# A two-layer graph network on one core: GpSimd's order written by hand in both layers, with the clearing of a short row at three places among the gathers of every group

## The chip, the cores and the metric

The kernel runs on one core of one Trainium2 chip. A core has five engines that work side by side, each on its own queue of instructions: TensorE (PE in the profile, with its weight loads as PEld), VectorE (DVE), ScalarE (ACT), GpSimd (POOL) and SyncE (SP), which issues most of the plain DMAs. GpSimd issues the indirect DMAs, the ones that fetch rows of a table by a list of row numbers. The metric is the device time of one execution in microseconds, and the time of a kernel is the median over its runs.

## The reference

There are 6250 nodes with 256 features and 200000 edges, each with a source node, a destination node and 128 features. The edges come sorted by destination. Two layers follow each other, each added to its input and normalised:

```python
edge_index = jnp.stack([src, dst])
x = _layernorm(x + _L0_gnn_ref(x, edge_index, edge_attr_128, W_edge, b_edge, W1, b1, W2, b2, eps, gamma, beta))
x = _layernorm(x + _L1_gnn_ref(x, W, att, src, dst))
```

The first layer makes a message for every edge, sums the messages by destination, and sends the sums through two dense layers and a normalisation over all nodes:

```python
msg = relu(x[src] + edge_attr @ W_edge + b_edge)
agg = segment_sum(msg, dst)
h = relu(((1 + eps) * x + agg) @ W1 + b1) @ W2 + b2
h = relu((h - mean(h)) * rsqrt(var(h) + 1e-5) * gamma + beta)
```

The second layer is attention with four heads. Every edge gets a logit from its two ends, the logits are made into weights by a softmax over the edges of one destination, and the weighted rows of the sources are summed:

```python
e = leaky_relu(es[src] + ed[dst])
alpha = exp(e - segment_max(e, dst)[dst]) / segment_sum(exp(...), dst)[dst]
out = segment_sum(alpha * z[src], dst)
```

So both layers need, for every edge, one row of a table of nodes: `x[src]` in the first, `z[src]` in the second.

## The kernel before

**Tiling.** The 200000 edges are cut into 1563 rows of 128 edges (`NSUB`), and 14 rows make a group (`S = 14`). There are 112 groups (`G`); the last has 9 rows. One row is fetched by one indirect DMA: 128 row numbers, one for each partition, and a table row for each. So each layer issues 1563 gathers on GpSimd.

**The first layer.** Rows are taken in pairs. `fetch` (L537 to L544, the gather itself at L542) takes a buffer `xg` from a pool of 14 and issues one or two gathers into it, from `in_x` in the first 20 groups and from `xb_tab`, a copy of `x` with the bias added, in all later ones. `features` multiplies the edge features by `W_edge` on TensorE into `pt`. `sums` (L556) adds the gathered rows on VectorE. `upper` (L561, ScalarE) and `lower` (L565, VectorE) make the relu in two parts, and `add_up` (L575) sums by destination with a one-hot matrix on TensorE. At the end of a group `flush` carries the sums through the dense layers. While groups 3 to 19 run, `biased` (L497 to L502) also writes `xb_tab` piece by piece: a load, an addition on VectorE (L500), a store.

**Between the layers.** `middle` finishes the normalisation, writes the tables `z_tab` and `ed_tab`, and uses GpSimd for a few additions (L727).

**The second layer.** `gather` (L877 to L886, the gather itself at L883) issues the gathers of one group into `ring`, which has room for four groups. The gathers of group i+1 stand in the program in front of the work on group i. `logits` (L951 to L963) needs the whole gathered group, and its first reader of it is the addition at L952. Then come maxima, the weights, and `weigh` (L1007 on VectorE, L1011 on TensorE), which multiplies the gathered rows by the weights and sums them by destination. `leave` normalises the finished rows and stores them; the last two groups are stored by an indirect DMA on GpSimd (L1039).

**What sets the order.** Both loops stand in a block whose engines run in the order in which the program is written:

```python
with tc.manual_schedule(engines={ET.DVE, ET.PE, ET.Activation, ET.SP}):
```

GpSimd (`ET.Pool`) is not in that set, so a planner orders its queue. In both loops GpSimd has nothing but the gathers and, at the very end, the two stores. An engine's instructions start in the order of its queue, and an instruction waits on semaphores for the buffers that it needs.

Of the kernel before, what the change touches and what calls it, by code (L numbers as in the profile page):

```python
# [6 lines left out]
F32 = mybir.dt.float32  # L7
# [6 lines left out]
ET = mybir.EngineType  # L14
# [18 lines left out]
XB_FROM = 20  # L33
RING = 4
XTB = 4
FIRST = 256
IN_RANGE = "the value is an id of a node, which the kinds of inputs bound"

# [10 lines left out]
def gnn(ctx, tc, io, N, E):  # L49
    nc = tc.nc  # L50
# [16 lines left out]
    const = ctx.enter_context(tc.tile_pool(name="const", bufs=1))  # L67
# [40 lines left out]
    nc.vector.memset(nil, 0.0)  # L108
    ones3 = const.tile([3, P], BF16, name="ones3")
    nc.vector.memset(ones3, 1.0)  # L110


    gf = const.tile([P, 2 * G], F32, name="gf")
# [325 lines left out]
    with ExitStack() as st:  # L439
# [97 lines left out]
        def fetch(k):  # L537
            g, j0, w = pairs_[k]
            XG[k] = gp.tile([P, 2, D], F32, tag="xg", name="xg")
            for i in range(w):  # L540
                t = gs[g] + j0 + i
                nc.gpsimd.indirect_dma_start(  # L542
                    out=XG[k][:, i, :], out_offset=None, in_=io["x"] if g < GB else xb_tab,
                    in_offset=bass.IndirectOffsetOnAxis(ap=src_sb[:, t:t + 1], axis=0))  # L544

        def features(k):
            g, j0, w = pairs_[k]
            pt = PT[k] = pe.tile([P, 2, D], F32, tag="pe", name="pt")
            for i in range(w):
                if g < GB:  # L550
                    nc.tensor.matmul(pt[:, i, :], ones3, bias3, start=True, stop=False)
                nc.tensor.matmul(pt[:, i, :], EA.pop(gs[g] + j0 + i), we_sb, start=not g < GB, stop=True)  # L552
# [32 lines left out]
            while chunks:  # L585
                yield from biased(chunks.pop(0))

        with tc.manual_schedule(engines={ET.DVE, ET.PE, ET.Activation, ET.SP}):
            def run(gen):
                for _ in gen:  # L590
                    pass

            run(positions(0, ldp))
            pieces(0)
            run(hot(0))
            load_rest()
            XW[0] = window(0)

            side = [positions(r, ldp) for r in range(1, len(parts))]
            rest = [first_table()]  # L600
            checks = [order(r, ldp) for r in range(len(parts))]
            hots, flushes = iter(()), []
            fill = zeros()
            extras = [place_rows(t0, pps, wk) for t0 in range(0, NSUB, P)]
            for f in (0, 1):
                if f < K:
                    fetch(f)
                    features(f)

            def step(queue):  # L610
                while queue:
                    if next(queue[0], True) is None:
                        return True
                    queue.pop(0)
                return False

            for k in range(K + 2):
                g = pairs_[min(k, K - 1)][0]
                if k < K and pairs_[k][1] == 0:
                    hots = hot(g + 1) if g + 1 < G else iter(())  # L620
                    if g % 2 == 0 and g + 2 < G:
                        pieces(g // 2 + 1)
                    if g + 1 < G:
                        XW[g + 1] = window(g + 1)
                    if g == GB - 1:
                        while step(rest):
                            pass
                j = k - firsts_[g] if k < K else 99
                if k + 2 < K:
                    fetch(k + 2)  # L630
                    features(k + 2)
                if k < K:
                    sums(k)
                    upper(k)
                    if 1 <= k:
                        lower(k - 1)
                elif k == K:
                    lower(k - 1)
                if k >= 2:
                    add_up(k - 2)  # L640
                    if k - 2 in lasts_:
                        run(fill)
                        gg = pairs_[k - 2][0]
                        flushes.append(flush(gg, ACC.pop(gg), XW.pop(gg)))
                        if gg > TG and extras:
                            flushes.append(extras.pop(0))
                if k == min(2, K - 1):
                    places_rest()
                if j >= 3:
                    next(hots, None)  # L650
                if k < K and pairs_[min(k + 1, K - 1)][0] != g:
                    run(hots)
                if k < 7:
                    next(fill, None)
                step(flushes)
                if len(flushes) > 1:
                    step(flushes)
                step(side)
                if 3 <= g < GB and k < K:
                    step(rest)  # L660
                    step(rest)
                if g >= GB:
                    step(checks)
                if k < K and g == TG and pairs_[k][1] == 0:
                    while step(side):
                        pass
                    while step(checks):
                        pass
                    flushes.append(tables(pps, wk))
                    extras = [break_columns(), break_rows(pps, wk)] + extras  # L670
            for q in (side, rest, checks, flushes, extras):
                while step(q):
                    pass
# [3 lines left out]
    def middle(h2T, stats):  # L677

        with ExitStack() as st:
# [28 lines left out]
            nc.sync.dma_start(ed_tab[NB * P:], zero[:, 0, :EW])  # L708
            cuts = [0] + [min(c0, NB * P) for c0 in range(FIRST, NB * P + CH, CH)]
            cs = list(zip(cuts, cuts[1:]))  # L710
            M = {}

            def load(ci):
                c0, c1 = cs[ci]
                xt = yp.tile([P, 2, CH], F32, tag="xt", name="xt", bufs=XTB)
                nc.sync.dma_start(xt[:, :, :c1 - c0], io["xT"].rearrange("(k p) n -> p k n", p=P)[:, :, c0:c1])
# [76 lines left out]
            none = iter(())  # L793
            for ci in range(min(XTB - 1, nch)):
                load(ci)
            with tc.manual_schedule(engines={ET.DVE, ET.PE, ET.Activation, ET.SP}):
                for i in range(nch + 3):
                    if i + XTB - 1 < nch:
                        load(i + XTB - 1)
                    a, b, d = (f(j) if 0 <= j < nch else none  # L800
# [45 lines left out]
    with ExitStack() as st:  # L846
# [30 lines left out]
        def gather(g):  # L877
            n = size(g)
            slot = T["slot"] if T["slot"] + n <= RING * S else 0
            T["slot"] = slot + n  # L880
            zg = ring[:, slot:slot + n]
            for j, t in enumerate(groups(g)):
                nc.gpsimd.indirect_dma_start(  # L883
                    out=zg[:, j, :], out_offset=None, in_=z_tab,
                    in_offset=bass.IndirectOffsetOnAxis(ap=src_sb[:, t:t + 1], axis=0))
            T["zg", g] = zg  # L886

        def loads(g):
# [155 lines left out]
            n = size(g)  # L1044
            return [(j, min(2, n - j)) for j in range(0, n, 2)]

        with tc.manual_schedule(engines={ET.DVE, ET.PE, ET.Activation, ET.SP}):
            gather(0)
            loads(0)
            loads(min(1, G - 1))  # L1050
            places(0)
            dst_parts(0)
            none = iter(())

            for i in range(G + 2):
                units = pairs(i - 1) if 1 <= i <= G else []
                hot = onehots(i) if i < G else none
                out = none
                if i + 1 < G:
                    gather(i + 1)  # L1060
                if 1 < i + 2 < G:
                    loads(i + 2)
                if 1 <= i <= G:
                    load_h(i - 1)
                    maxima(i - 1)
                if i + 1 < G:
                    places(i + 1)
                next(hot, None)

                def some(k):  # L1070
                    for _ in range(min(k, len(units))):
                        weigh(i - 1, *units.pop(0))

                some(1)
                if i < G:
                    logits(i)
                some(1)
                if i >= 2:
                    carry(i - 2)
                    out = leave(i - 2)  # L1080
                if i + 1 < G:
                    dst_parts(i + 1)
                some(1)
                next(out, None)
                some(1)
                if i < G:
                    rows_between(i)
                next(hot, None)
                some(1)
                next(out, None)  # L1090
                some(1)
                for _ in out:
                    pass
                some(len(units))
                for _ in hot:
                    pass
# [217 lines left out]
```

## Time and profile before

| what | value |
|---|---|
| median of 11 runs | 4111.64 us (4105.77 to 4126.58) |
| the profiled execution, its own time | 4113.03 us |
| its span, first to last instruction | 4111.2 us |
| PE busy | 2944.6 us, 72% of the span |
| DVE busy | 3178.8 us, 77% |
| ACT busy | 1041.9 us, 25% |
| POOL busy | 3010.8 us, 73%, 3158 instructions |
| first gather of the first layer starts | 3.0 us |
| last gather of the first layer starts | 1992.6 us |
| first gather of the second layer starts | 2099.1 us |
| last gather of the second layer starts | 4069.6 us |

The table's last four rows are starts of instructions in the trace, in microseconds from the start of the span. A busy time is the sum of an engine's instructions; an engine that is less than fully busy can still be the one that sets the pace, if the rest of its time is a fixed pause between instructions. In the lists of groups a line reads: source line, engine, operation, what is written and read, shapes, count, then busy time and mean duration in nanoseconds of one, then the idle time in front of these instructions and what ended it. In a timeline a line reads: start and duration in microseconds, engine, line, operation, and in brackets the idle time before it with what ended that. A list of waits gives, for an engine, what waited for what: microseconds in total, times, and the longest one.

### The profile page before, as it was taken

How to read it: one execution, taken by the hardware profiler on the slowest of the kernel's cores; microseconds unless marked ns; L12 is line 12 of the kernel's file. 1: busy time of each engine (PE TensorE's matmuls, PEld its weight loads, DVE VectorE, ACT ScalarE, POOL GpSimd, SP SyncE). 2: the span in 40 equal slices, each digit the busy share in tenths (PEclk: the TensorE clock that was granted, in tenths of full speed). 3: DMA queues.
4: the chain of work that ended last, by engine and by line, in shares of the span. 5: the costliest groups of instructions: out<-in, count | busy, mean ns of one | idle time of the engine just before them, and what ended most of it. 6: DMA issues, size and time to landing. Idle time of an engine off the chain costs nothing. (4 is left out here: it accounts for less than half of the span.)

```text
span 4111.2 us, 49111 instructions
## 1 busy us (share of the span) xinstructions
PE 2944.6 (72%) x12883; PEld 2001.8 (49%) x12883; DVE 3178.8 (77%) x8203; ACT 1041.9 (25%) x3046; POOL 3010.8 (73%) x3158
## 2 busy tenths in 40 slices
PE   7899787777777777777746666666666666666665
PEld 4456665556665666665533433333333343333333
DVE  6677988877777777777757777778777777777787
ACT  3233333333333333333421111111111111111111
POOL 7567777777777777777557777777777777777774
PEclk9799999998999999999877777777777777777777
DMA  6755655555555555555565555555555555555553
GB/s 204 220 165 169 196 173 169 169 166 172 167 161 162 160 165 167 167 167 163 158 167 150 144 149 151 151 150 145 149 150 150 151 150 145 150 151 151 150 147 94
DMA packets 298029, 656.24 MB, mean 160 GB/s; under 512 B 86827, under 2 KB 170139, under 8 KB 290572
## 3 DMA queue, kind: packets, MB, share of 16 engines
q0 software_dynamic: 150144, 416.54, 36.4%
q1 hardware_dynamic: 146090, 235.43, 16.9%
q8 instruction: 106, 1.74, 0.2%
q14 instruction: 183, 1.50, 0.1%
q10 hardware_dynamic: 1506, 1.04, 0.1%
HBM read 617.82 MB, written 34.99 MB: 159 GB/s over the span
## 5 line engine op out<-in xcount | busy, mean ns | idle before, releaser
L883 POOL DMA_INDIRECT ring<-z_tab,src_sb x1563 | 1495.6, 957 | 495.7 <-issue 293.6
L542 POOL DMA_INDIRECT xg<-xb_tab,src_sb x1283 | 1214.9, 947 | 390.9 <-issue 274.8
L1011 PE MATMUL acc<-y,oh 128*128 128x260 f32 x3126 | 1071.4, 477 | 296.9 <-DVE y L1007 295.8
L552 PE MATMUL pt<-we_sb,ea_t 128*128 128x256 f32 x3126 | 946.3, 420 | 308.0 <-DVE hl L565 302.5
L1011 PEld LDWEIGHTS acc<-y,oh 128*128 128x128 f32 x3126 | 645.2, 228 | 541.5 <-DVE y L1007 460.7
L552 PEld LDWEIGHTS pt<-we_sb,ea_t 128*128 128x128 f32 x3126 | 563.8, 201 | 515.6 <-DVE hl L565 201.6
L561 ACT ACTIVATE hl<-pt 128x512 fp32r<-128x512 f32 x782 | 466.8, 597 | 1070.0 <-DVE pt L556 966.4
L556 DVE TENSOR_TENSOR pt<-pt,xg 128x512 f32<-128x512 f32 x782 | 542.0, 693 | 218.1 <-DMA xg<-xb_tab,src_sb 200.8
L575 PE MATMUL acc<-hl,oh 128*128 128x512 f32 x1563 | 668.6, 510 | 1.9 <-DVE hl L565 1.9
L565 DVE SCALAR_TENSOR_TENSOR hl<-pt,hl 128x512 fp32r<-128x512 f32 x782 | 532.9, 682 | 0.0
L1007 DVE TENSOR_TENSOR y<-ring,cst 128x520 f32<-128x520 f32 x782 | 527.8, 675 | 0.6 <-PE acc L1011 0.4
L542 POOL DMA_INDIRECT xg<-in_x,src_sb x280 | 265.8, 949 | 121.5 <-issue 64.5
L575 PEld LDWEIGHTS acc<-hl,oh 128*128 128x128 f32 x1563 | 312.8, 200 | 50.1 <-DVE hl L565 2.6
L962 PE MATMUL tr<-consts,top 128*4 128x128 f32 x112 | 41.5, 371 | 398.8 <-DVE top L944 398.8
L952 DVE TENSOR_TENSOR e<-e,ring 128x56 f32<-128x56 f32 x112 | 28.6, 255 | 347.5 <-DMA ring<-z_tab,src_sb 277.0
L1023 ACT COPY ag<-acc 128x260 f32<-128x260 f32 x111 | 41.6, 375 | 875.8 <-DVE acc L1020 875.1
L523 DVE TENSOR_TENSOR oh<-iota_p,dloc 128x896 fp32r<-128x896 f32 x224 | 241.5, 1078 | 0.0
L933 DVE TENSOR_TENSOR oh<-cst,dloc 128x896 f32<-128x896 f32 x224 | 239.3, 1068 | 0.2 <-ACT cst L993 0.2
L962 PEld LDWEIGHTS tr<-consts,top 128*4 128x4 f32 x112 | 9.2, 82 | 458.3 <-issue 440.7
L414 DVE SCALAR_TENSOR_TENSOR pmk<-p,mk 128x128 f32<-128x128 f32 x224 | 56.3, 289 | 126.6 <-ACT h2T L404 125.4
L400 PEld LDWEIGHTS p<-r,w_sb 128*128 128x128 f32 x896 | 137.4, 220 | 13.8 <-ACT r L395 1.7
L390 PE MATMUL p<-hw,w_sb 128*128 128x128 f32 x896 | 127.0, 288 | 22.8 <-DVE carry L472 22.1
(219 smaller groups left out, 3060.2 us busy)
## 6 DMA issues: line engine op xcount, KB each, us to landing
ea_t<-in_eaT SPq DMA_DIRECT2D x54, 1792.0 KB
dlb<-dl_tab SPq DMA_DIRECT2D x111, 448.0 KB
ring<-z_tab,src_sb POOLq DMA_INDIRECT x1563
xg<-xb_tab,src_sb POOLq DMA_INDIRECT x1283
xw<-in_x SPq DMA_DIRECT2D x112, 128.0 KB
hw<-hT_tab SPq DMA_DIRECT2D x112, 128.0 KB
out<-o SPq DMA_DIRECT2D x110, 128.0 KB
xr<-in_x SPq DMA_DIRECT2D x24, 256.0 KB
```

The source lines that it names most:

```text
L400: nc.tensor.matmul(p2[:, m, :], w2_sb[:, k, m * P:(m + 1) * P], r1[:, k, :], start=(k == 0), stop=(k == 1))
L523: nc.vector.tensor_tensor(OH[g][:, c0:c1], iota_p.unsqueeze(1).to_broadcast([P, c1 - c0, P]), dl.unsqueeze(2).to_broadcast([P, c1 - c0, P] ...
L542: nc.gpsimd.indirect_dma_start(out=XG[k][:, i, :], out_offset=None, in_=io["x"] if g < GB else xb_tab, in_offset=bass.IndirectOffsetOnAxis ...
L552: nc.tensor.matmul(pt[:, i, :], EA.pop(gs[g] + j0 + i), we_sb, start=not g < GB, stop=True)
L556: nc.vector.tensor_add(PT[k][:, :w], PT[k][:, :w], XG.pop(k)[:, :w])
L561: nc.scalar.activation(HL[k][:, :w, 0], PT[k][:, :w], AF.Relu)
L565: nc.vector.scalar_tensor_tensor(HL[k][:, :w, 1], PT.pop(k)[:, :w], 0.0, HL[k][:, :w, 0].bitcast(F32), op0=OP.max, op1=OP.subtract)
L575: nc.tensor.matmul(ACC[g].rearrange("p a d -> p (a d)"), OH[g][:, j0 + i], hl[:, i].rearrange("p a d -> p (a d)"), start=(j0 + i == 0), st ...
L883: nc.gpsimd.indirect_dma_start(out=zg[:, j, :], out_offset=None, in_=z_tab, in_offset=bass.IndirectOffsetOnAxis(ap=src_sb[:, t:t + 1], axi ...
L933: nc.vector.tensor_tensor(T["oh", g][:, c0:c1], iota_p.unsqueeze(1).to_broadcast([P, c1 - c0, P]), dloc[:, gs[g] + c0:gs[g] + c1].unsqueez ...
L1007: nc.vector.tensor_tensor(y[:, :w], T["zg", g][:, j0:j0 + w, :ZW].rearrange("p s (h f) -> p s h f", f=F + 1), by_edge(T["ex", g], g)[:, j0 ...
L1011: nc.tensor.matmul(T["acc", g].rearrange("p h f -> p (h f)"), T["oh", g][:, j0 + i, :], y[:, i].rearrange("p h f -> p (h f)"), start=(j0 + ...
```

## The change

GpSimd joins the engines whose order is that of the program, in both layers. A new tile of one partition and 768 float32 values is set to zero on GpSimd after the gathers of rows 4, 9 and 13 of every group (rows are counted from 0). Nothing reads this tile.

```diff
+RESTS = (4, 9, 13)
...
+    rest_t = const.tile([1, 768], F32, name="rest_t")
+
+    def breathe():
+
+        nc.gpsimd.memset(rest_t, 0.0)
...
                 nc.gpsimd.indirect_dma_start(
                     out=XG[k][:, i, :], out_offset=None, in_=io["x"] if g < GB else xb_tab,
                     in_offset=bass.IndirectOffsetOnAxis(ap=src_sb[:, t:t + 1], axis=0))
+                if j0 + i in RESTS:
+                    breathe()
...
-        with tc.manual_schedule(engines={ET.DVE, ET.PE, ET.Activation, ET.SP}):
+        with tc.manual_schedule(engines={ET.DVE, ET.PE, ET.Activation, ET.SP, ET.Pool}):
...
                 nc.gpsimd.indirect_dma_start(
                     out=zg[:, j, :], out_offset=None, in_=z_tab,
                     in_offset=bass.IndirectOffsetOnAxis(ap=src_sb[:, t:t + 1], axis=0))
+                if j in RESTS:
+                    breathe()
...
-        with tc.manual_schedule(engines={ET.DVE, ET.PE, ET.Activation, ET.SP}):
+        with tc.manual_schedule(engines={ET.DVE, ET.PE, ET.Activation, ET.SP, ET.Pool}):
```

## The prediction

> **What bounds the kernel now.** I read the page's groups of instructions first, to see which engine carries the layers; then GpSimd's timeline, for its pace; then busy times by stretch, to hold that pace against the whole span; then the lists of waits, to see who waits for whom. The page's groups:
>
> ```profile
> L883 POOL DMA_INDIRECT ring<-z_tab,src_sb x1563 | 1495.6, 957 | 495.7 <-issue 293.6
> L542 POOL DMA_INDIRECT xg<-xb_tab,src_sb x1283 | 1214.9, 947 | 390.9 <-issue 274.8
> L542 POOL DMA_INDIRECT xg<-in_x,src_sb x280 | 265.8, 949 | 121.5 <-issue 64.5
> ```
>
> POOL is busy for only 73% of the span, less than DVE (77%), but nearly all of it is gathers of 0.95 us, each with idle time put down to "issue". The timeline at the start of the second layer shows what that is:
>
> ```profile
> 2078.19 1.00 POOL L727 TENSOR_TENSOR hn<-hn,xt 128x384 f32<-128x384 f32 x1 [1.66 <-ACT hn L725]
> 2099.09 0.96 POOL L883 DMA_INDIRECT ring<-z_tab,src_sb  x1 [19.91 <-DMA pen<-pen_tab]
> 2100.36 0.95 POOL L883 DMA_INDIRECT ring<-z_tab,src_sb  x1 [0.30 <-issue]
> 2101.61 1.16 POOL L883 DMA_INDIRECT ring<-z_tab,src_sb  x1 [0.30 <-issue]
> 2103.07 0.95 POOL L883 DMA_INDIRECT ring<-z_tab,src_sb  x1 [0.30 <-issue]
> ```
>
> A gather is 0.95 us and a pause of 0.30 us, 1.25 us from start to start, from the second gather of the layer on, straight after 19.91 us without a gather. So the pace is not set by a queue that has filled up. The busy times by stretch (engine, busy microseconds, count) say that it holds:
>
> ```profile
> 100.00:236.00 136.00, 114.11 (x414) 68.85 (x413) 89.03 (x186) 34.77 (x90) 77.33 (x82) 0.81 0.66 209
> 236.00:1994.00 1758.00, 1388.85 (x6285) 1066.13 (x6284) 1389.17 (x3057) 638.46 (x1645) 1329.82 (x1405) 0.94 0.52 167
> 2099.00:4071.00 1972.00, 1275.77 (x5515) 754.36 (x5515) 1533.54 (x4392) 273.09 (x1096) 1495.61 (x1563) 0.74 0.54 149
> ```
>
> POOL is the fifth pair of numbers. From 236 to 1994 us it issues 1405 gathers, one per 1.251 us; from 2099 to 4071 us 1563, one per 1.262 us. In these 3730 us of the 4111.2 it pauses for nothing but its own 0.30, while DVE is busy for 79% and 78%. Only from 100 to 236 us is it held up, with 82 gathers where 1.25 us each would give 109. The waits of DVE over the whole span agree:
>
> ```profile
> DVE e L952 <- DMA ring<-z_tab,src_sb: 277.0, 86, 11.5
> DVE pt L556 <- DMA xg<-xb_tab,src_sb: 200.8, 102, 6.1
> ```
>
> DVE's two longest waits are for gathered rows. GpSimd's queue sets the pace of both layers, and what is added to it lengthens the span. The exception, POOL's waits from 100 to 236 us:
>
> ```profile
> POOL xg L542 <- DVE pt L556: 39.5, 19, 5.0
> ```
>
> Nineteen gathers waited for a buffer that DVE had not read yet: 39.5 us, of which 19 x 0.30 = 5.7 are the usual pause, so 33.8 us of slack.
>
> **The change part by part.** *Order by hand.* Inside both blocks POOL has the gathers and two stores; they stay in one queue in the program's order, and no DMA of SP or of POOL is moved past another. Nothing in the trace shows a different planner's order being paid for or saved. Best case, it removes the 33.8 us and the 19.91 us before the second layer: -54 us. Worst, one more pause of 0.30 us per group: 224 x 0.30 = +67 us. I take 0, because POOL runs at its bare pace everywhere else; what hides it is that buffers are free long before they are needed, and without that the 67 us would show.
>
> *The clearings.* Rows 4, 9 and 13 exist in 111 groups of 14; the last group has 9 rows, so only row 4. That is 111 x 3 + 1 = 334 per layer, 668 in all. Behind each one the rest of the layer's gathers are queued, and DVE (L556, L952) waits for those.
>
> The trace shows no clearing of this length on POOL. The nearest rows:
>
> ```profile
> 0.25 0.10 POOL L1301 MEMSET const-float32-0.0<- 128x1 f32 x1 [0.25 <-issue]
> 0.28 0.10 POOL L1301 MEMSET const-float32-1.0<- 128x1 f32 x1
> 0.31 0.11 POOL L1301 MEMSET const-bfloat16-1.0<- 128x1 bf16 x1
> 0.34 0.12 POOL L1301 MEMSET const-uint8-127<- 128x1 uint8 x1
> ```
>
> ```profile
> L304 DVE MEMSET pen<- 112x387 f32 x1 | 0.4, 381 | 0.0
> L861 DVE MEMSET down<- 4x129 f32 x3 | 0.5, 166 | 0.0
> ```
>
> ```profile
> L727 POOL TENSOR_TENSOR hn<-hn,xt 128x512 f32<-128x512 f32 x22 | 29.0, 1323 | 27.7 <-ACT hn L725 18.8 <-DVE rr L331 8.9
> L727 POOL TENSOR_TENSOR hn<-hn,xt 128x256 f32<-128x256 f32 x2 | 1.4, 716 | 22.7 <-ACT hn L725 22.7
> ```
>
> On DVE a MEMSET takes (381 - 166) / (387 - 129) = 0.83 ns per element, with 4 partitions or 112, so one partition saves nothing: 768 x 0.83 = 0.64 us. POOL's own one-element memsets take 0.10 to 0.12 us. Together 0.74 us, which I take: same operation, POOL's own start. An upper end is POOL's addition, (1323 - 716) / 256 = 2.37 ns per element plus 0.11: 1.93 us; but it reads two operands for each element written, and a clearing reads none, so I hold it unlikely. The lower end is 0.10 us, if length costs nothing. As to the pause: POOL's four memsets start 0.03 us apart, with no pause, so the 0.30 belongs to the gathers and I keep it, once per gather. If a clearing had one of its own, 0.74 becomes 1.04; if it ran inside the gather's, 0.44.
>
> [...]
>
> *Where the clearings lie.* Gathers up to 236 us: 78 by 100 us and 82 after, 160, that is 11 groups and 6 rows, 3 x 11 + 1 = 34 clearings. DVE's pace decides when those gathers end, and POOL has 33.8 us of slack there: 34 x 0.74 = 25.2 us fit in. Without that cover they would cost 25 us more. The other 634 lie where POOL never waits: 634 x 0.74 = 469 us. The stretch between the layers (1994 to 2099 us) and the end behind the last gather (4071 to 4111 us) keep their length. DVE and PE have room: a second-layer group goes from 14 x 1.262 = 17.7 to 19.9 us, of which DVE works 13.7.
>
> Sum: the profiled execution took 4113.0 us, 1.9 around its span and 1.4 above the median of 4111.6. 4113.0 + 469 = 4582 us.
>
> **The rivals.**
>
> *The clearing runs in the gather's pause.* If the 0.30 is the tail of a gather and POOL can clear meanwhile, 0.44 is left: 634 x 0.44 = 279, 4392 us. For it: ordinary POOL instructions start without a pause. Against: the next instruction waits through those 0.30 us even when all that it needs is there.
>
> *The same, with a clearing that is cheap: faster.* If the clearing takes the pause's place and costs only 0.10 us as the one-element rows do, each saves 0.20: 634 x 0.20 = 127, 3986 us. It turns to a gain where a clearing is shorter than 0.30 us and the pause is not repeated. Against: MEMSET grows with length on DVE, and a pause that a rest could remove should also be missing at 2100.36 us, right after 19.91 us of rest; it isn't.
>
> *Hidden altogether.* The clearing lies on a part of GpSimd that gathers do not need fully; the pace stays at 1.25 us, 4113 us. For it: only one of 128 partitions is touched. Against: in all of this trace nothing runs on POOL beside a gather.
>
> *Dear.* Priced by POOL's addition: 668 x 1.93 = 1289, less the 33.8 of slack, 5368 us. For it: it is the only long instruction of POOL in the trace. Against: three streams against one.
>
> **How the numbers follow.** Forecast (0.55 to 1.05 us each, 634 of them: 4460 to 4780 us) 0.66; inside the pause 0.12; dear 0.12, with prices between 1.05 and 1.93; hidden 0.06; faster 0.04. The range runs from 0.37 us (634 x 0.37 = 235, 4350) to 1.21 us (767, 4880): below it lie hidden and faster, above it most of dear, together under 0.2. About 0.2% is what a measurement of this kernel can tell from no change, 8 us. Faster by more than that: the faster rival, and 0.01 of the hidden one, where the hand order also removes the early waits, 0.05; within it, the rest of the hidden one, 0.05; slower, the other three, 0.90.
>
> **What would show it.** POOL gets 668 MEMSET rows, and from each gather of rows 4, 9 and 13 to the next gather it takes 1.25 + 0.74 = 1.99 us from start to start, all others 1.25. A second-layer group takes 17.7 + 2.2 = 19.9 us. The waits of DVE L952 and L556 for gathered rows grow by some 470 us together, DVE's share falls to 69%, and POOL's waits for L556 before 236 us all but disappear. The price of the one clearing makes or breaks the number: each 0.1 us of it is 63 us. If the gathers behind a clearing came closer together than 1.25 us, or the start-to-start time there stayed at 1.25, I would be wrong in kind and not only in size.

## The result, and the profile after

The changed kernel takes 4503.93 us (median of 8 runs, 4501.06 to 4509.07). The kernel before, run again on the same chip, takes 4115.63 us (31 runs). The ratio is 1.0943, with a 95% interval of 1.093 to 1.0957: 388 us slower. The profiled execution took 4506.15 us, its span 4504.3 us. That is inside the predicted range of 4350 to 4880 us, and 78 us below the predicted 4582.

The page's groups of GpSimd, after (line, engine, operation, shapes, count, then busy time, mean nanoseconds of one, and idle time in front):

```profile
L892 POOL DMA_INDIRECT ring<-z_tab,src_sb x1563 | 1514.3, 969 | 448.4 <-issue 299.0
L549 POOL DMA_INDIRECT xg<-xb_tab,src_sb x1283 | 1216.9, 949 | 351.8 <-issue 238.8
L549 POOL DMA_INDIRECT xg<-in_x,src_sb x280 | 267.0, 954 | 96.2 <-issue 55.9
L117 POOL MEMSET rest_t<- 1x768 f32 x668 | 486.4, 728 | 0.1
```

The 668 clearings are there, 0.728 us each, with no idle time in front of them. The gathers of the second layer (L892) are 12 ns longer than before, and all gathers have less idle time in front of them. GpSimd's timeline, after, in the second layer, shows why:

```profile
3008.76 0.94 POOL L892 DMA_INDIRECT ring<-z_tab,src_sb  x1 [0.30 <-issue]
3010.01 0.95 POOL L892 DMA_INDIRECT ring<-z_tab,src_sb  x1 [0.30 <-DVE rd L370]
3010.95 0.73 POOL L117 MEMSET rest_t<- 1x768 f32 x1
3011.84 0.95 POOL L892 DMA_INDIRECT ring<-z_tab,src_sb  x1 [0.16 <-issue]
3013.10 0.95 POOL L892 DMA_INDIRECT ring<-z_tab,src_sb  x1 [0.30 <-DMA ring<-z_tab,src_sb]
```

The clearing starts where the gather ends (3010.01 + 0.95 = 3010.96), and the next gather starts 0.16 us behind it and not 0.30. From gather to gather it is 1.832 us around a clearing and 1.251 us elsewhere (medians over the trace). So a clearing adds 0.581 us, which is 0.147 us less than its own 0.728.

Busy time by stretch, after (the fifth pair is POOL), and the waits that answer to those of before:

```profile
111.00:240.00 129.00, 105.25 (x381) 62.93 (x381) 82.06 (x169) 31.94 (x82) 90.09 (x99) 0.82 0.64 203
240.00:2175.00 1935.00, 1422.15 (x6283) 1080.44 (x6282) 1397.67 (x3057) 637.89 (x1645) 1549.01 (x1705) 0.92 0.47 151
2280.00:4466.00 2186.00, 1278.62 (x5520) 754.16 (x5520) 1542.74 (x4400) 275.83 (x1099) 1755.97 (x1897) 0.72 0.49 134
```

```profile
DVE e L963 <- DMA ring<-z_tab,src_sb: 445.9, 89, 13.0
DVE pt L565 <- DMA xg<-xb_tab,src_sb: 330.7, 163, 6.3
```

```profile
POOL xg L549 <- DVE pt L565: 21.3, 16, 4.7
```

DVE's work is nearly unchanged (1397.67 against 1389.17 us, 1542.74 against 1533.54) in longer stretches, and its waits for gathered rows grew from 277.0 and 200.8 to 445.9 and 330.7 us: 299 us of the 393 by which the span grew. POOL's waits for buffers in the first 240 us (last line) are 21.3 us; in the first 236 us of before they were 39.8 us.

The 393.1 us can be added up from the starts of the gathers in the two traces. First layer, first to last gather: 1989.6 to 2170.0, +180.4. Between the layers: 106.5 to 107.4, +0.9. Second layer: 1970.5 to 2183.5, +213.0. The rest, before the first and behind the last gather: -1.2.

- Second layer: 334 x 0.581 = 194.1, and 1563 gathers that are 12 ns longer, 18.7. Together 212.8.
- First layer: 334 x 0.581 = 194.1, less what the clearings took out of POOL's waits for buffers. Idle time beyond the usual pause, summed over the first 200 gathers, fell from 34.1 to 17.0 us, so -17.1. The gathers' own duration grows from 1480.7 to 1483.9, 3.2. Together 180.2.

The 12 ns are a few long gathers: 154 of 1563 in the second layer take over 1.0 us, 98 before. Of these 154, 104 overlap DVE's L922 (L911 before), the one-hot of the places, 1792 bfloat16 elements per partition. Of all gathers that overlap it, 104 of 113 are long after, but only 56 of 187 before, so the overlap alone doesn't make a gather long. What the two traces share is the order of the starts: of the gathers that start up to 0.4 us behind the start of this DVE instruction, 42 of 46 are long before and 66 of 67 after. With the clearings more gathers fall there; why isn't shown. The timeline after shows a long one:

```profile
3018.11 0.89 DVE L922 TENSOR_SCALAR ohT<-dlb,consts 128x1792 bf16<-128x1792 bf16 x1
3018.68 1.14 POOL L892 DMA_INDIRECT ring<-z_tab,src_sb  x1 [0.16 <-issue]
```

The gather above starts 0.57 us behind L922's start, later than the 0.4 us of that count, and 0.32 us before L922 ends; it takes 1.14 us and not 0.95. What holds such a gather up the traces don't show, and no run here took L922 away.

### The profile page after: what moved, and what is told of

Same layout as the page of the kernel before. It is cut to its first block, busy times and chain, and to the rows that moved or that the text cites. A ratio compares the mean times of both kernels' runs of the same rounds, so it can differ in the third digit from the quotient of the medians.

```text
span 4504.3 us, 49779 instructions
## 1 busy us (share of the span) xinstructions
PE 2980.4 (66%) x12883; PEld 2014.7 (45%) x12883; DVE 3195.6 (71%) x8203; ACT 1043.2 (23%) x3046; POOL 3516.1 (78%) x3826
## 3 DMA queue, kind: packets, MB, share of 16 engines
q8 instruction: 106, 1.74, 0.2%
## 5 line engine op out<-in xcount | busy, mean ns | idle before, releaser
L892 POOL DMA_INDIRECT ring<-z_tab,src_sb x1563 | 1514.3, 969 | 448.4 <-issue 299.0
L1022 PE MATMUL acc<-y,oh 128*128 128x260 f32 x3126 | 1074.8, 478 | 303.7 <-DVE y L1018 302.7
L561 PE MATMUL pt<-we_sb,ea_t 128*128 128x256 f32 x3126 | 962.0, 426 | 455.5 <-DVE hl L574 448.8
L1022 PEld LDWEIGHTS acc<-y,oh 128*128 128x128 f32 x3126 | 645.4, 229 | 549.6 <-DVE y L1018 467.9
L565 DVE TENSOR_TENSOR pt<-pt,xg 128x512 f32<-128x512 f32 x782 | 542.8, 694 | 364.9 <-DMA xg<-xb_tab,src_sb 330.7
L584 PE MATMUL acc<-hl,oh 128*128 128x512 f32 x1563 | 677.9, 516 | 2.2 <-DVE hl L574 2.2
L117 POOL MEMSET rest_t<- 1x768 f32 x668 | 486.4, 728 | 0.1
L963 DVE TENSOR_TENSOR e<-e,ring 128x56 f32<-128x56 f32 x112 | 28.9, 258 | 552.3 <-DMA ring<-z_tab,src_sb 445.9
```

Of the source, the lines that this page charges most:

```text
L117: nc.gpsimd.memset(rest_t, 0.0)
L565: nc.vector.tensor_add(PT[k][:, :w], PT[k][:, :w], XG.pop(k)[:, :w])
L584: nc.tensor.matmul(ACC[g].rearrange("p a d -> p (a d)"), OH[g][:, j0 + i], hl[:, i].rearrange("p a d -> p (a d)"), start=(j0 + i == 0), st ...
L892: nc.gpsimd.indirect_dma_start(out=zg[:, j, :], out_offset=None, in_=z_tab, in_offset=bass.IndirectOffsetOnAxis(ap=src_sb[:, t:t + 1], axi ...
L1022: nc.tensor.matmul(T["acc", g].rearrange("p h f -> p (h f)"), T["oh", g][:, j0 + i, :], y[:, i].rearrange("p h f -> p (h f)"), start=(j0 + ...
```

## The experiments

All experiments ran on four chips on which the kernel before takes longer than on the chip of the result: 5124.36, 5133.20, 5194.25 and 5132.99 us, not 4115.63. Every ratio below is against the kernel before on the same chip. That the times differ so much was not foreseen; it decides the sign, as the changed kernel's own run there shows. The record of the result names no chip, and no experiment ran beside it, so whether it is the chip itself or something else that was different at that time is not shown; "the chip of the result" and "these chips" stand for the two cases. What a trace shows of a single clearing, from one gather to the next in a stretch where nothing else waits, can be compared across chips: a gather after a gather starts after 1.25 us on all of them.

The theory at the start: the clearings are serial work on the queue that sets the pace, less 0.14 us of the pause in front of the next gather. The rivals: the hand order has a price or a gain of its own; a clearing has a fixed cost; a clearing of one partition runs beside the gathers, as the prediction's "hidden altogether" has it.

### The order alone, one element, another partition, one behind every gather

Order by hand, no clearing:

```diff
-RESTS = (4, 9, 13)
+RESTS = ()
```

> GpSimd's order by hand in both layers, no clearing anywhere. If the whole loss is the clearings (668 x 0.58 us from start to start of the gathers around one, 1.83 against 1.25), this takes as long as the kernel before: 4112 us, within 10. If the hand order has a price or a gain of its own, it shows here alone: a gain could be at most the 33.8 us of early waits and the 19.9 us before the second layer, so 4060; a price would be what 668 x 0.58 = 388 doesn't cover, a few us.

Measured: 5117.57 against 5124.36 us, ratio 0.9985 (0.9965 to 1.0004). The order by itself makes no difference here. On these chips GpSimd waits for long (982 us, below), which would hide a small price on its queue; for the chip of the result the evidence is the sum above, which leaves 0.2 us of each layer to anything but the clearings and the gathers' duration. The absolute numbers expected were those of another chip.

One element at the same places:

```diff
-    rest_t = const.tile([1, 768], F32, name="rest_t")
+    rest_t = const.tile([1, 1], F32, name="rest_t")
```

> The same three places, but the row has one element. The changed kernel's trace has no pause in front of a clearing and 0.16 us behind it, where a gather after a gather has 0.30. If the clearing takes the place of 0.14 us of that pause whatever its length, one of 0.10 us makes the way from gather to gather 0.95 + 0.10 + 0.16 = 1.21 us, 0.04 less than without it: 634 x 0.04 = 25 us faster than before, 4088 us. If the gather needs its 0.30 us whatever stands behind it, and a clearing only runs in it, the way stays 1.25 us and the time is that of before, 4112 us. If a clearing has a cost that doesn't depend on its length, the time stays well above, 4200 us or more.

Measured: 5117.18 us, ratio 0.9992 (0.9975 to 1.0009): no difference. From gather to gather around such a clearing it is 1.251 us.

One element behind every gather:

```diff
-RESTS = (4, 9, 13)
+RESTS = tuple(range(14))
...
-    rest_t = const.tile([1, 768], F32, name="rest_t")
+    rest_t = const.tile([1, 1], F32, name="rest_t")
```

> A clearing of one element behind every gather, 1563 in each layer. If a clearing takes the place of part of the pause, every gather comes 0.04 us earlier: 3126 x 0.04 = 125 us less, 3990 us. If it only runs in the pause, 4112 us. If each clearing has a cost of its own that doesn't depend on length, such as 0.1 us, 4400 us.

Measured: 5142.57 us, ratio 1.0035 (1.0016 to 1.0055): 18 us for 3126 clearings, 6 ns each. GpSimd's timeline of this kernel:

```profile
3000.05 0.94 POOL L892 DMA_INDIRECT ring<-z_tab,src_sb  x1 [0.22 <-issue]
3000.99 0.09 POOL L117 MEMSET rest_t<- 1x1 f32 x1
3001.30 0.95 POOL L892 DMA_INDIRECT ring<-z_tab,src_sb  x1 [0.22 <-DVE oh L944]
3002.24 0.09 POOL L117 MEMSET rest_t<- 1x1 f32 x1
3002.55 0.95 POOL L892 DMA_INDIRECT ring<-z_tab,src_sb  x1 [0.22 <-issue]
```

A one-element clearing takes 0.09 us, the pause behind it is then 0.22 us, and the next gather still starts 1.25 us after the last (median 1.251). So the pause is not replaced, as my expectation of 25 us gained had it. The gather keeps its 1.25 us, and this clearing of 0.09 us is free, where the one of 0.728 us adds 0.581, its duration less some 0.147 us. The rival of a fixed cost falls, and so does the faster one of the prediction; it is the way from gather to gather that decides both, as the total time here is not set by GpSimd.

The same length on partition 64:

```diff
-    rest_t = const.tile([1, 768], F32, name="rest_t")
+    rest_t = const.tile([P, 768], F32, name="rest_t")
...
-        nc.gpsimd.memset(rest_t, 0.0)
+        nc.gpsimd.memset(rest_t[64:65], 0.0)
```

> The same clearing of 768 elements, but on partition 64 and not on partition 0. If GpSimd does one instruction after another whatever the partition, the time is that of the changed kernel, 4504 us. [...]

Measured: 4887.65 us, ratio 0.9541 (0.9511 to 0.9571), faster than before. The expectation did not have that. The timeline of this kernel excludes that the clearing ran beside the gathers:

```profile
3005.07 0.94 POOL L892 DMA_INDIRECT ring<-z_tab,src_sb  x1 [0.30 <-issue]
3006.01 0.73 POOL L117 MEMSET rest_t<- 1x768 f32 x1
3006.90 1.02 POOL L892 DMA_INDIRECT ring<-z_tab,src_sb  x1 [0.16 <-issue]
```

From gather to gather it is 1.83 us, as with partition 0. So longer work on GpSimd's queue made this program faster on this chip, and that needed the next runs.

### The changed kernel itself, and the partition and the length

The changed kernel, with no edit:

> The changed kernel itself, beside the kernel before on the chip of these runs. The first four runs were on a chip where the kernel before takes 5124 us and not 4116, and the clearing on partition 64 took 0.954 of that time. Theory A, GpSimd's queue sets the pace: wherever the kernel before takes about 4115 us, this takes 1.094 of it. Theory B, on a chip where something else than GpSimd sets the pace the clearings are hidden or even help: where before takes about 5124 us, this takes about 0.954 of it, like the clearing on partition 64. If the partition decided it, this would take 1.05 or more on that chip too.

Measured: 4886.33 against 5133.20 us, ratio 0.9531 (0.9495 to 0.9567). Theory B holds: on this chip the change is 4.7% faster, where it was 9.4% slower on the chip of the result.

Partition 64 again, the edit as above:

> The clearing of 768 elements on partition 64 again. In its first trace the way from gather to gather around a clearing was 1.83 us, as in the changed kernel with partition 0. So it should take what the changed kernel takes on the same chip, ratio to it 1.00; if the part of GpSimd that has the partition mattered, the two would differ by some per cent, with the one on partition 64 the faster.

Measured: 4881.13 us, ratio 0.9521 (0.9472 to 0.957), the changed kernel's within the intervals. The partition makes no difference, and the rival of a clearing beside the gathers falls for the two partitions tried.

Half the length:

```diff
-    rest_t = const.tile([1, 768], F32, name="rest_t")
+    rest_t = const.tile([1, 384], F32, name="rest_t")
```

> The row has 384 elements and not 768. The trace of the changed kernel has a clearing of 0.727 us and the one of one element took 0.088 us, so 0.84 ns per element, and 384 take 0.41 us. If the first 0.146 us of a clearing run in the gather's pause and the rest is added, the way between two gathers around one is 1.25 + 0.41 - 0.146 = 1.51 us, and on a chip where before takes 4115 us the sum is 634 x 0.26 = 167 us more, ratio 1.04. If instead half of a clearing is hidden, whatever its length, it is 1.25 + 0.20 = 1.45 us and 1.03.

Measured: 0.407 us each and 1.513 us from gather to gather (medians), as the first account has it (1.51) and not the second (1.45). The time is 5007.25 us, ratio 0.9757 (0.972 to 0.9793), half of the gain.

All partitions:

```diff
-    rest_t = const.tile([1, 768], F32, name="rest_t")
+    rest_t = const.tile([P, 768], F32, name="rest_t")
```

> The clearing on all 128 partitions, 768 elements each. If GpSimd clears all partitions side by side, a clearing takes 0.73 us and the time is the changed kernel's. If one partition is a special, cheaper case, it takes longer: at twice the duration 1.46 us each, 668 x 0.73 = 488 us more.

Measured: 0.757 us each, 0.03 more than with one partition, from gather to gather 1.86 us; 4952.64 us, ratio 0.9656 (0.9611 to 0.9701). 128 partitions cost nearly what one costs. That it gains less than one partition is not explained.

### What is different on these chips

The kernel with the order alone stands for the kernel before on these chips (ratio 0.9985). Its longest waits, DVE's first and then GpSimd's:

```profile
DVE fin L376 <- remote: 603.9, 90, 8.7
DVE pmk L421 <- ACT h2T L411: 445.6, 105, 9.5
DVE pt L565 <- PE acc L584: 158.0, 33, 7.2
```

```profile
POOL xg L549 <- DVE pt L565: 607.4, 187, 7.6
POOL ring L892 <- DVE frs L332: 331.7, 75, 5.1
```

DVE hardly waits for gathered rows here (16 us), and GpSimd waits for DVE to free buffers. In the timeline ("remote" is an update of a semaphore that the profile can give to no instruction):

```profile
3005.33 0.38 PE L359 MATMUL rows<-consts,hw 128*128 128x128 f32 x2
...
3006.74 1.15 PE L1022 MATMUL acc<-y,oh 128*128 128x260 f32 x4
3007.17 0.95 POOL L892 DMA_INDIRECT ring<-z_tab,src_sb  x1 [0.30 <-issue]
3008.42 0.94 POOL L892 DMA_INDIRECT ring<-z_tab,src_sb  x1 [0.30 <-issue]
3009.46 0.48 DVE L376 SCALAR_TENSOR_TENSOR fin<-rows,edw,fin 128x256 f32<-128x256 f32 x1 [3.14 <-remote]
```

DVE's L376 needs the rows that TensorE made by 3005.71 us, starts at 3009.46, and from 3007.89 (3006.74 + 1.15) until then no engine but GpSimd is at work. What these waits have in common can be read from the semaphores in the trace: every wait of DVE and ScalarE that is shown as "remote" is for the semaphore that TensorE's instructions raise. It is raised, in the middle case, 3.4 us behind the end of TensorE's last recorded matmul. There are 821 us of such waits on DVE and 568 us on ScalarE, and none at all in the two traces from the chip of the result.

I counted in the traces all stretches of over 1.5 us in which none of the five engines starts an instruction, register and semaphore instructions included; these are called standstills below. The stretch in the timeline above is not one of them, since a gather starts in it. The fifth column is GpSimd's idle time beyond its usual pauses over the whole kernel, the last one the "remote" waits of DVE and ScalarE together.

| kernel | chip's time before | time | standstills (their sum, us) | GpSimd idle beyond pauses, us | late semaphore of TensorE, us |
|---|---|---|---|---|---|
| before, chip of the result | 4116 | 4116 | 5 (16) | 34 | 0 |
| changed, chip of the result | 4116 | 4504 | 4 (12) | 17 | 0 |
| order alone | 5124 | 5118 | 151 (467) | 982 | 1389 |
| changed | 5133 | 4886 | 40 (82) | 354 | 1138 |

GpSimd's 982 us account for the distance of the order alone from the chip of the result: 5114.2 - 4111.2 = 1003 us of span. With the clearings 354 us are left, and 668 x 0.58 = 388 us were added: 982 - 354 - 388 = 240 us gained, against 5114.2 - 4894.6 = 220 between the two spans. So the clearings are not merely hidden in waiting that was there anyway, which would give a ratio of 1.00; with them there is less waiting. The fall of the standstills from 151 to 40 overstates this, because a clearing is itself a start of GpSimd and a slower queue runs on for longer while the others wait: without GpSimd's starts the stretches are 203 (889 us) and 144 (514 us).

### Is it the mean rate of the gathers?

A clearing of 219 elements behind every gather:

```diff
-RESTS = (4, 9, 13)
+RESTS = tuple(range(14))
...
-    rest_t = const.tile([1, 768], F32, name="rest_t")
+    rest_t = const.tile([1, 219], F32, name="rest_t")
```

> The same addition to each group's gathers, in small pieces: a clearing of 219 elements behind every gather, 0.088 + 218 x 0.00084 = 0.27 us each, so the way from gather to gather is 1.25 + 0.27 - 0.146 = 1.375 us instead of 1.25 four times and 1.83 once. 14 x 0.125 = 1.75 us per group, the same as the changed kernel's 3 x 0.58 = 1.74. If only the mean rate of the gathers counts on a chip where before takes about 5125 us, the ratio is the changed kernel's 0.953, within 0.01. If single long rests are what lets something drain there, this stays near 1.00. On a chip where before takes 4115 us: 1.094 or more, as GpSimd's queue is then the pace.

Measured: 1.380 us from gather to gather; 5004.28 against 5194.25 us, ratio 0.9633 (0.9602 to 0.9663). The gain is 3.7% where the three long rests gained 4.7% on another of these chips, so long single rests are not needed for most of it. There are 43 standstills (82 us), but that is no evidence, as GpSimd starts twice as many instructions here as with the order alone; without its starts there are 198 (775 us), nearly as many as with the order alone.

The three clearings in one place:

```diff
-RESTS = (4, 9, 13)
+RESTS = (13,)
...
-        nc.gpsimd.memset(rest_t, 0.0)
+        for _ in range(3):
+            nc.gpsimd.memset(rest_t, 0.0)
```

> The three clearings of a group one after the other behind row 13. The added time per group is 3 x 0.73 - 0.146 = 2.04 us instead of 1.74. If only the mean rate counts on a chip where before takes about 5125 us: ratio about 0.95. If short stretches of gathers at full pace are what helps (5, 5 and 4 in the changed kernel, 14 here): clearly above it, 0.98 or more.

Measured: 5061.79 us, ratio 0.972 (0.9644 to 0.9797), 47 standstills, 139 us. Between the two expectations: some 2% less gain than with three places. The way around the three is 3.41 us, so they add 2.16 us per group and not 1.74. The mean rate is most of the gain, and where the rests lie is a part.

Twice at each place:

```diff
-        nc.gpsimd.memset(rest_t, 0.0)
+        for _ in range(2):
+            nc.gpsimd.memset(rest_t, 0.0)
```

> The row is cleared twice at each of the three places: 2 x 0.73 - 0.146 = 1.31 us added, the way between two gathers around it 2.56 us. GpSimd's queue alone then needs 4111 + 634 x 1.31 = 4942 us, a ratio of 0.964 on a chip where before takes 5125 us. If slower gathers keep removing the stretches in which the whole core stands still, the time comes down to that floor, 4942 to 5000 us; if those stretches remain as they are with one clearing (the changed kernel is 4886 there, 382 above its own floor of 4504), it is about 5320, ratio 1.04.

Measured: 5027.64 us, ratio 0.9679 (0.9649 to 0.9709), 6 standstills, 14 us. They are gone, and so are the "remote" waits (0). The two clearings take 1.51 us together and the way around them is 2.615 us, so 1.364 us is added and the floor is 4111 + 634 x 1.364 = 4976 us: GpSimd's queue sets the pace again, 52 us from it.

One and a half times:

```diff
         nc.gpsimd.memset(rest_t, 0.0)
+        nc.gpsimd.memset(rest_t[:, :384], 0.0)
```

> At each of the three places the row is cleared and then half of it again: 0.73 + 0.41 - 0.146 = 0.99 us added. GpSimd's queue alone then needs 4111 + 634 x 0.99 = 4739 us. With one clearing the time was 382 us above the queue's own 4504, with two 84 above 4942. If the stretches in which the whole core stands still fall off evenly between, this is about 4739 + 230 = 4970 and no better than one clearing; if they are nearly gone as with two, 4739 + 100 = 4840, faster than one clearing (4886) and than before (5125 to 5194), ratio 0.935 to 0.945. On a chip where before takes 4115 us: 1.15.

Measured: 4885.60 us, ratio 0.9522 (0.9502 to 0.9541), 3 standstills, 8 us, and 5 us of "remote" waits. The expectation that the standstills would be nearly gone holds, the time of 4840 us does not: it is no better than one clearing. The way around the two is 2.43 us, so 1.18 us is added and not 0.99, and GpSimd's queue alone needs 4111 + 634 x 1.18 = 4859 us. The two instructions are 0.79 us apart from start to start (0.06 more than the first lasts), and where one or the other lasts longer or a full 0.30 us pause follows, more is lost:

```profile
3012.74 0.73 POOL L117 MEMSET rest_t<- 1x768 f32 x1
3013.53 0.41 POOL L118 MEMSET rest_t<- 1x384 f32 x1
3014.24 0.95 POOL L893 DMA_INDIRECT ring<-z_tab,src_sb  x1 [0.30 <-issue]
```

In this kernel the waits of DVE are again those of the chip of the result, for gathered rows:

```profile
DVE e L964 <- DMA ring<-z_tab,src_sb: 512.9, 86, 14.2
DVE pt L566 <- DMA xg<-xb_tab,src_sb: 481.6, 237, 7.0
```

So between one clearing and one and a half the gain from less waiting and the price on GpSimd's queue balance, on these chips. The "remote" waits with no clearing, one of half the length, one, one and a half, and two are 1389, 1225, 1138, 5 and 0 us; with one element, which takes nothing from the gathers' rate, they are 1366 (three places) and 1552 us (behind every gather). They sink slowly up to one clearing and are all but gone at one and a half; the versions ran on different ones of the four chips. Of these only the one clearing ran on the chip of the result; each of the others would cost there what it adds between the gathers, an estimate from the sum above.

Why TensorE's semaphore comes late on these chips, and why slower gathers end it, stays open. Slower work of DVE or of the DMAs isn't seen: DVE's largest groups take 693, 682 and 677 ns with the order alone and 693, 682 and 676 ns before, and a packet takes 161 against 160 ns for GpSimd's DMAs and 76 ns in both for SyncE's. TensorE's clock is lower (0.776 granted against 0.840) and L1022 takes 523 ns a matmul and not 477; whether that is cause or consequence no run tells, but two clearings at each place end the late updates at a clock of 0.792. SyncE's register instructions are slow too: 153 of 1344 take over 0.5 us with the order alone and 203 in the changed kernel on these chips, 5 before. In the standstills of the order alone GpSimd's gathers go on moving data (29 packets per us, as over the whole span), while the packets of SyncE's DMAs nearly stop (3 per us, 29 over the span), which may be only because SyncE waits for the others. No run separates the possible causes. The traces of these chips also lack records of updates (2318 of TensorE's 2802 are there with the order alone, 2798 before), so it isn't excluded that the recording itself has a part in the delay.

## Why the prediction was right

**What bounds the kernel: right on the chip it was made from, by its own steps.** GpSimd's gathers paced both layers, 1.25 us each, and what was put into its queue lengthened the span. It doesn't hold on the chips of the experiments, where GpSimd is idle for 982 us beyond its pauses, most of it waiting for DVE. The profile of before could not show that; the prediction named no such case.

**Order by hand, 0 us:** right. The order alone is 0.9985, and on the chip of the result the stretch between the layers changed by 0.9 us. Whether the rests need it was not tried: nothing depends on a clearing, so an order that doesn't follow the program might put it elsewhere.

**The price of a clearing, 0.74 us:** right, 0.728. DVE's 0.83 ns per element and POOL's own start gave it; the runs' own slope is (0.728 - 0.088) / 767 = 0.83 ns. That DVE's price would hold for GpSimd was an assumption that came true, and the two rows of DVE differed in length and in partitions at once, so they could not show that partitions don't count. The runs show it: 0.757 us for 128 partitions.

**The pause kept once per gather, so that 0.74 is added: the step that failed.** Some 0.146 us of the pause is given up when a clearing stands in front of a gather, so 0.58 is added. This is the term that was mis-sized: 634 x 0.74 = 469 us should have been 634 x 0.58 = 368 us. The rival "the clearing runs in the gather's pause" was half right; it had all 0.30 us covered, 0.44 added. The faster rival falls with the one-element runs: the way from gather to gather stays 1.25 us.

**The 34 clearings that fit into early slack:** right in kind, too large. They took 17.1 us out of POOL's waits, of 34 x 0.581 = 19.8; the prediction had 25.2. POOL's waits did not all but disappear, 21.3 us are left.

**What the prediction did not have:** longer gathers, 18.7 + 3.2 = 21.9 us; of the long ones in the second layer 104 of 154 lie beside DVE's L922. With them 668 x 0.581 = 388.1, less 17.1, plus 21.9 is 392.9 against 393.1 measured. So of the 469 us predicted 76 were too many: 101 from the pause, less these 22 us and 3 us of cover that wasn't there. That the two made the first smaller is luck.

**Hidden altogether, dear:** both fall. Partition 64 costs what partition 0 costs (1.83 us around it), and the clearing has DVE's price per element (0.83 ns), not that of POOL's additions (2.37 ns).

**The signs named beforehand:** from gather to gather 1.99 us around a clearing was foreseen and 1.83 seen; a second-layer group of 19.9 us, seen 2183.5 x 14 / 1563 = 19.6; 470 us more waiting at L952 and L556, seen 299; a DVE share of 69%, seen 71%.

## What to carry to other kernels

An engine that is busy for 73% can be the bound: look at the way from start to start of its instructions, and ask whether the rest is a pause that nothing else fills. Here a clearing of 0.728 us between two gathers cost its duration less 0.147 us of a 0.30 us pause, and one of 0.088 us cost nothing (1.251 us from gather to gather with it and without); in another kernel, measure that part with the shortest instruction there is. And before a rest is called a loss or a gain, time it on the chips that the kernel will run on: the same 668 clearings cost 9.4% in one place and gained 4.7% in another. In these two cases the lists of waits of the kernel without clearings told them apart, by whether DVE waits for gathered rows or GpSimd for DVE.

## What the runs showed of the hardware

- The kernel before takes 4116 us in the runs of the result and 5124 to 5194 us on the four chips of the experiments. The difference is idle time of GpSimd (982 us with the order alone, against 34), behind waits for TensorE's semaphore that end, in the middle case, 3.4 us after TensorE's last recorded matmul (1389 us on DVE and ScalarE, against none). With 0.73 + 0.41 us of clearing at three places per 14 gathers these waits are 5 us.
- A gather on GpSimd takes 1.25 us from start to start, 0.95 of it busy; a clearing of 0.407, 0.728 or 0.757 us behind it adds its duration less some 0.146 us.
- A clearing on GpSimd takes 0.088 us for one element, 0.407 for 384 and 0.728 for 768, with one partition; 0.757 for 768 with 128 partitions.
- A gather that starts up to 0.4 us behind DVE's `tensor_scalar` on 1792 bfloat16 elements takes over 1.0 us instead of 0.95 in 42 of 46 cases before and 66 of 67 after; the one in the lines shown, 0.57 us behind, takes 1.14 us.
